# Moving a relu, a set of block sums and a row maximum by one place in the written order of a one-core graph-network kernel

## The chip, the cores and the metric

The kernel runs on one core of one Trainium2 chip. The metric is the device time of one execution in microseconds (us). A core has engines that run side by side, each through its own list of instructions: TensorE multiplies matrices (PE in the profile; PEld is the loading of its stationary operand), VectorE works elementwise (DVE), ScalarE does copies, exponentials and other activations (ACT), GpSimd does small work here (POOL), and SyncE issues the DMA transfers (SP). They wait for each other through semaphores.

## The reference

Two layers run over 16 graphs ("batches") of 1,024 nodes with 512 features. Layer 0 is an adjacency product and a weight product, layer 1 a graph attention with a masked softmax. Both start with a layer norm and a relu and end in a residual.

```
def _layernorm(x, axis=-1, eps=1e-5):
    m = jnp.mean(x, axis=axis, keepdims=True)
    v = jnp.var(x, axis=axis, keepdims=True)
    return (x - m) / jnp.sqrt(v + eps)

# --- layer 0 ---
h = jnp.maximum(_layernorm(x, axis=-1), 0.0)
y = jnp.einsum('nm,bmd->bnd', adj, h)
x = x + (jnp.einsum('bnd,do->bno', y, weight) + bias)
# --- layer 1, mask = adj ---
u = jnp.maximum(_layernorm(x, axis=-1), 0.0)
h = jnp.einsum('bnc,cf->bnf', u, W)
s1 = jnp.einsum('bnf,f->bn', h, a[:F, 0])
s2 = jnp.einsum('bnf,f->bn', h, a[F:, 0])
e = jax.nn.leaky_relu(s1[:, :, None] + s2[:, None, :], negative_slope=0.2) * mask
att = jax.nn.softmax(e, axis=2)
x = x + jax.nn.elu(jnp.einsum('bij,bjf->bif', att, h) + beta * h)
```

Shapes: x (16, 1024, 512), adj and mask (1024, 1024), weight and W (512, 512), all float32. (The reference calls both normed inputs h; u is the kernel's name for the second.)

## The kernel before

**Products.** Every matrix product is split into 2 x 2 blocks and done with seven block products instead of eight (Strassen's scheme in Winograd's form, `PRODUCTS`): p1 to p7, whose left operands are A11, A12, A22 and the sums S1 to S4, and whose right operands are B11, B21, B22 and the sums T1 to T4. The results are accumulated in three kinds of PSUM banks, Y, W and X. In layer 0, from batch 1 on, each of the seven products is split once more into seven inner products r1 to r7 (`inner_steps`, line 197). Their left sums are made on VectorE by `inner_left` (line 435), four additions of 128 x 256 each; they are the `in_p` tiles. In the trace r1, r6 and r7 of product p3 are the matmuls that write `y_p3y`, and r5 shares their PSUM tile `yx`: r1, r6 and r7 use its first half, r5 its second half. After r1 ScalarE copies the first half out (`y_p3t`), after r5 it copies the second half into the left sums' tile (`in_p`), and after r6 VectorE adds these two (`y_p3t<-y_p3y,in_p`); r7 writes the first half anew. The names are the same for p7, p4 and, in layer 1 where only p4 is split again, for `z_p4y` and `z_p4t`.

**Layer 0** (`layer0_a2`, line 451, through `products_a2`, line 300) runs for each batch in 28 steps, numbered 0 to 27. Products go in pairs, p1 with p2 (steps 0 to 6), p6 with p5 (7 to 13), p7 with p3 (14 to 20), then p4 with the first weight product woven in (21 to 27); then the other six weight products follow (`po_Y`, `po_X`, `po_W` in the trace). In a pair the two products' inner products alternate, two to a step: p7 r1, p7 r2 | p3 r1, p7 r5 | p3 r2, p7 r4 | p3 r5, p7 r6 | p3 r4, p7 r3 | p3 r6, p7 r7 | p3 r3, p3 r7. In the first step of a pair the last results of the pair before are read out (the list `behind`): for p5 these are two ScalarE copies of the X banks (`y_C<-y_X`).

**Side work.** After step k of a batch, `after(k)` issues whatever a table lists for k. For layer 0 the table is `plan_out` (line 1151) merged with others. It finishes the previous batch: the residual rows (`xr`) are normalized into u, statistics (`o.stats`), relu (`o.relu`, two ScalarE activations of 128 x 512 in place), the attention logits (`o.logits`, VectorE), and the stores. `inner_left` of p7, p3 and p4 and the loads of residual rows stand in the same table. `plan_norm_a` adds the next batch's norm statistics (`h_stats`, ScalarE, from step 15 on).

**Layer 1** (`layer1`, line 910, through `products_a`, line 275) takes 12 half-product steps 0 to 11 (p1, p2, p6, p5, p7, p3 with two steps each), then p4 in seven steps with a weight product woven in, then the other weight products (`pq_*`). Beside batch b's products runs the softmax of batch b+1 (`SOFTMAX_A`, line 1202): `M` masks a row block on VectorE and takes its maxima, `X` sends the maxima through DRAM to the other partitions (`mall`), `N` takes the first half's maxima from them (`top`, two small VectorE instructions that make `nm`), `E` is the exponential on ScalarE, which needs `nm`, and `V` transposes on VectorE. `LATE_A` (line 1209) makes T3 and T4, the last right sums of batch b: VectorE additions of 128 x 1024, one for each half, "a" and "b". p7 reads T3, p4 reads T4. In batch 0 `w_sums` makes the sums of the second weight matrix, four additions of 128 x 512.

**Order.** All engines are wrapped in `InOrder` (line 111), which keeps the order of the program on each of them; a table entry's place therefore is its place in the queue of each engine that it uses. `merged` (line 1119) appends the plans' entries for one step in the order in which the plans are passed.

Of the kernel before, what the change touches and what calls it, by code (L numbers as in the profile page):

```python
# [66 lines left out]
def kernel(  # L67
# [34 lines left out]
    def bank(name):  # L102
        return psum.tile([P, 512], F32, tag="ps", name=name)
# [232 lines left out]
    class Weighted:  # L336
# [17 lines left out]
        def steps(self, n, left):  # L354

            prod, _, bn, kind, first, last = self.products[n]
            first = first and (kind, 0) not in self.banks

            def step(q, i, dc):
                if first and i == 0 and dc == 0:  # L360
                    self.banks[kind, q] = bank(f"{self.name}_{kind}{q}")
                ps = self.banks[kind, q].rearrange("p (i o) -> p i o", i=2)
                pe.matmul(
                    ps[:, i, :], left[:, dc, ts(2 * q + i, P)], self.w[:, W_BLOCK[bn], dc, :],
                    start=(first and i == 0 and dc == 0), stop=(last and dc == 1),
                    skip_group_check=True,
                )
                if i and dc:
                    self.done(prod, q, ps)

            return [partial(step, q, i, dc) for q in range(2) for i in range(2) for dc in range(2)]
# [10 lines left out]
    def load_w(name, src):  # L382

        w = const.tile([P, 7, 2, HD], F32, tag="w", name=name)
        for i in range(2):
            for j in range(2):
                sp.dma_start(
                    out=w[:, 2 * i + j],
                    in_=src[ts(i, HD), ts(j, HD)].rearrange("(c p) o -> p c o", p=P),
                )  # L390
        return w
# [727 lines left out]
    def merged(*plans):  # L1119
        out = {}  # L1120
        for plan in plans:
            for k, steps in plan.items():
                out.setdefault(k, []).extend(steps)
        return out
# [26 lines left out]
    def plan_out(o, b):  # L1151

        return steps(
            (-1, o.keep, 0, 1), (-1, o.keep, 1, 0), (-1, o.keep, 1, 1), (0, o.relu, 0, 0),
            (1, o.stats, 1, 0, 0), (3, o.relu, 0, 1), (4, o.stats, 1, 0, 1), (7, o.relu, 1, 0),
            (8, o.stats, 1, 1, 0), (10, o.stats, 1, 1, 1), (13, o.relu, 1, 1),
            (2, o.logits, 0, 0, 0), (3, o.logits, 0, 0, 1), (7, o.logits, 0, 1, 0),
            (8, o.logits, 0, 1, 1), (9, o.logits, 1, 0, 0), (10, inner_left, b, "p7"),
            (12, o.logits, 1, 0, 1), (13, inner_left, b, "p3"), (15, o.logits, 1, 1, 0),
            (16, o.logits, 1, 1, 1), (16, o.store_logits), (18, inner_left, b, "p4"),  # L1160
            (3, o.store, 0, 0), (6, o.store, 0, 1), (10, o.store, 1, 0), (15, o.store, 1, 1),
            (18, begin, b, "Y"), (24, begin, b, "X"),
            (8, load_res, b, 0, 0), (10, load_res, b, 0, 1), (14, load_res, b, 1, 0),
            (18, load_res, b, 1, 1),
        )
# [16 lines left out]
    def plan_softmax(order, s):  # L1182
        names = {
            "L": [s.logits], "B": [s.blocks, 0], "b": [s.blocks, 1],
            "X": [s.spread_max, 0], "x": [s.spread_max, 1], "N": [s.top, 0], "n": [s.top, 1],
            "S": [s.spread_sum, 0], "s": [s.spread_sum, 1],
            "D": [s.diagonal, 0], "d": [s.diagonal, 1],
        }
        for g in range(NCH):
            names[f"M{g}"] = [s.masked, g]  # L1190
            names[f"E{g}"] = [s.exp, g]
            names[f"V{g}"] = [s.turn, g]
            names[f"L{g}"] = [s.load, g]
            names[f"e{g}"] = [s.load, g, b4, "b4"]
            names[f"K{g}"] = [s.keep, g]
            names[f"R{g}"] = [s.reload, g]
        for n in ("T1", "T2", "T3", "T4"):
            for k in range(2):
                names[n + "ab"[k]] = [s.right_sum, n, k]
        return {k: [tuple(names[n]) for n in steps.split()] for k, steps in order.items()}  # L1200
# [5 lines left out]
    }  # L1206
    SOFTMAX_B = {1: "D", 2: "T1a", 3: "T1b", 4: "d", 5: "T2a", 6: "T2b"}
    LOGITS_B = {8: "L", 9: "L0", 10: "L1", 11: "e2", 12: "e3"}
    LATE_A = {5: "T3a T4a", 6: "T3b T4b"}


    EARLY_B = {
# [18 lines left out]
    sms = [Softmax(b) for b in range(B)]  # L1231
    out_of = None
    for b in range(B):
        plans = [plan_out(out_of, b)] if b else []
        plans_b = []
        if b + 1 < B:
# [21 lines left out]
        if b == 0:  # L1258
            plan_b = merged(
                {  # L1260
                    0: [(logit_weights_back, 0), (logit_weights_back, 1)],
                    1: [(inner_right, "p7", 1)], 2: [(inner_right, "p3", 1)],
                    3: [(inner_right, "p4", 1)],
                },
                *plans_b,
            )
            layer0_a(b, merged(plan_first(), at_end(merged(*plans))))
        else:
            plan_b = merged(*plans_b)
# [9 lines left out]
    w1_c = load_w("w1_c", w1)  # L1279
    for b in range(B):  # L1280
        plans = [{
            k - 14: [(f,) for f in later.pop(k)] for k in sorted(later)
        }]
        plans.append(plan_softmax(LATE_A, sms[b]))
        plans.append(steps((7, p4_right, b, 0), (8, p4_right, b, 1), (8, p4_left, b)))
        plans.append(steps((3, u_sums, b, 0, 1), (4, u_sums, b, 1, 1)))
        plan_b = {}
        if b == 0:
            plans += [
                {6: [(w_sums, w1_c)]}, steps((-1, u_sums, b, 0, 0), (0, u_sums, b, 1, 0)),  # L1290
            ]
        if b + 1 < B:
            plans.append(plan_softmax(SOFTMAX_A, sms[b + 1]))
            plans.append({k: [(load_u, b + 1, n)] for k, n in LOADS_U.items()})
            plan_b = plan_softmax(SOFTMAX_B, sms[b + 1])
        else:
            plans.append({7 + i: [(load_x1, b, nh, q)] for i, (nh, q) in enumerate(halves)})
        if b + 2 < B:
            plan_b = merged(plan_b, plan_softmax(LOGITS_B, sms[b + 2]))
        if 1 <= b <= NCH:  # L1300
            plan_b = merged(plan_b, {
                4: [(late.load, b - 1)], 9: [(late.stats,)], 10: [(late.relu,)],
                11: [(late.logits, b - 1)], 13: [(late.store,)],
            })
            if b == NCH:
                plan_b[13].append((late.store_logits,))
        if b + 1 < B:
            plan_b = merged(plan_b, steps((10, u_sums, b + 1, 0, 0), (12, u_sums, b + 1, 1, 0)))
        plans.append({18: plan_b.pop(1, [])})
        layer1(b, merged(*plans), plan_b)  # L1310
    for k in sorted(later):
        for f in later[k]:
            f()
# [33 lines left out]
```

## Time and profile before

| quantity | before |
|---|---|
| time, median of 3 runs | 2254.78 us (2254.56 to 2255.46) |
| the profiled execution's own time | 2254.63 us |
| its span, first to last instruction | 2252.7 us |
| PE busy | 2236.1 us, 99% |
| PEld, DVE, ACT, POOL busy | 73%, 87%, 69%, 11% |
| granted TensorE clock | 0.998 |
| DMA, mean | 149 GB/s |

The span leaves out 1.93 us of the execution around the program's instructions. Times in the trace are counted from the start of the span. All instructions carry line 119, that of the wrapper `InOrder`, so that they are told apart by their tiles: what is written stands left of the arrow, what is read right of it, with buffer numbers left out. A matmul row "x4" is one inner product. In square brackets is the time that the engine stood idle before a row, and what ended it.

### The profile page before, as it was taken

To read this page: it belongs to the slowest core of one execution; us is meant where nothing else is said; L and a number is where in the kernel's file an instruction comes from. 1 tells how busy PE (TensorE), PEld (TensorE's weight loads), DVE (VectorE), ACT (ScalarE), POOL (GpSimd) and SP (SyncE) were. 2 spreads that over 40 slices of the span, in tenths; PEclk is the share of its full clock that TensorE was granted. 3 is DMA by queue.
4 is the path that set the end of the run, shared out by engine and by line. 5 is a ranking of instruction groups with operands and counts; after the bars stand their busy time and mean duration, and the time that the engine had idled before them with its cause. 6 is when DMAs were issued, how large, how long until landed. Compare 5 with 4: busy or idle time off the path is not lost.

```text
span 2252.7 us, 30436 instructions
## 1 busy us (share of the span) xinstructions
PE 2236.1 (99%) x8716; PEld 1645.5 (73%) x8716; DVE 1950.3 (87%) x4477; ACT 1547.9 (69%) x4138; POOL 243.7 (11%) x508
## 2 busy tenths in 40 slices
PE   9999999999999999999999999999999999999998
PEld 5888888888888888888666556665666556665565
DVE  7888888998888998898989988898889988888864
ACT  3766766676777676776576777768777776767743
POOL 1211111111111111111000000000000000000000
PEclk9999999999999999999999999999999999999999
DMA  7433454443444343344535665465554655446541
GB/s 210 140 126 119 160 171 132 141 140 117 148 160 151 134 142 120 120 150 159 202 110 175 165 169 166 145 196 156 164 168 149 191 142 153 139 143 165 159 120 49
DMA packets 194296, 336.07 MB, mean 149 GB/s; under 512 B 78800, under 2 KB 86992, under 8 KB 194128
## 3 DMA queue, kind: packets, MB, share of 16 engines
q1 hardware_dynamic: 185168, 302.15, 41.2%
q0 software_dynamic: 8640, 31.46, 7.5%
q8 instruction: 68, 1.11, 0.2%
q14 instruction: 100, 0.82, 0.1%
q10 hardware_dynamic: 320, 0.52, 0.1%
HBM read 228.33 MB, written 109.91 MB: 150 GB/s over the span
## 4 chain that ended last, share of the span: by engine, by line
PE 96%; DVE 2%; ACT 1%; DMA 1%; issue 0%; POOL 0%; SPq 0%; DVEq 0%; POOLq 0%
PE z_Y L119 16%; PE po_Y L119 10%; PE pq_Y L119 9%; PE z_X L119 9%; PE y_Y L119 8%; PE po_X L119 5%; PE z_W L119 5%; PE pq_X L119 5%; PE y_X L119 4%; PE y_W L119 3%; PE y_p7y L119 2%; PE pq_W L119 2%; PE po_W L119 2%; PE z_p4y L119 2%; PE y_p3y L119 2%; PE y_p4y L119 2%
## 5 line engine op out<-in xcount | busy, mean ns | idle before, releaser
L119 ACT ACTIVATE e<-e,nm 128x256 f32<-128x256 f32 x480 | 236.8, 498 | 51.4 <-DVE nm L119 51.4
L119 DVE CUSTOM_DVE_ANT_0 e<-e,mask 128x256 f32<-128x256 f32 x512 | 199.9, 424 | 54.0 <-ACT e L119 52.8
L119 PE MATMUL z_Y<-pT,ul_U 128*128 128x512 f32 x512 | 224.9, 592 | 0.0
L119 ACT ACTIVATE e<-s2b,s1b 128x256 f32<-128x256 f32 x512 | 214.7, 500 | 0.0
L119 PE MATMUL pq_Y<-w_c,z_C 128*128 128x256 f32 x768 | 189.1, 379 | 0.0
L119 PE MATMUL po_Y<-w_c,y_C 128*128 128x256 f32 x768 | 188.3, 379 | 0.0
L119 PEld LDWEIGHTS z_Y<-pT,ul_U 128*128 128x128 f32 x512 | 97.3, 190 | 115.6 <-issue 111.5
L119 DVE CUSTOM_DVE_ANT_0 y_S<-xr,v_bc 128x512 f32<-128x512 f32 x240 | 165.3, 689 | 9.2 <-DVE s L119 0.5
L119 PEld LDWEIGHTS po_Y<-w_c,y_C 128*128 128x128 f32 x768 | 145.9, 190 | 20.3 <-ACT po_X L119 0.2
L119 PEld LDWEIGHTS pq_Y<-w_c,z_C 128*128 128x128 f32 x768 | 145.9, 190 | 19.9
L119 DVE STREAM_TRANSPOSE pT<-e 128x512 f32<-128x512 f32 x240 | 150.8, 680 | 1.5
L119 ACT ACTIVATE h<-h,nb_h,r_h 128x512 f32<-128x512 f32 (+1 forms) x132 | 98.2, 792 | 57.1 <-POOL nb_h L119 57.1
L119 ACT ACTIVATE y_S<-xr 128x512 f32<-128x512 f32 x90 | 56.7, 630 | 91.9 <-DVE xr L119 91.5
L119 POOL DMA_DIRECT2D o<-x1d x60 | 52.7, 935 | 609.7 <-DVE o L119 546.8
L119 PE MATMUL pq_X<-w_c,z_S 128*128 128x256 f32 x512 | 115.9, 379 | 0.0
L119 PE MATMUL po_X<-w_c,y_S 128*128 128x256 f32 x512 | 115.7, 379 | 0.0
L119 PE MATMUL z_W<-pT,ul_U 128*128 128x512 f32 x256 | 112.5, 592 | 0.0
L119 PE MATMUL z_Y<-pT_T,ul_S 128*128 128x512 f32 x256 | 112.5, 592 | 0.0
L119 PE MATMUL z_X<-pT_T,ul_S 128*128 128x512 f32 x256 | 112.5, 592 | 0.0
L119 PE MATMUL z_X<-pT,ul_S 128*128 128x512 f32 x256 | 112.5, 592 | 0.0
L119 PEld LDWEIGHTS pq_X<-w_c,z_S 128*128 128x128 f32 x512 | 96.3, 190 | 14.5 <-DVE z_C L119 0.8
L119 PEld LDWEIGHTS po_X<-w_c,y_S 128*128 128x128 f32 x512 | 97.3, 190 | 13.2
(259 smaller groups left out, 5238.3 us busy)
## 6 DMA issues: line engine op xcount, KB each, us to landing
mask<-maskd SPq DMA_DIRECT2D x128, 512.0 KB
h<-in_x_dram SPq DMA_DIRECT2D x64, 512.0 KB
xr<-in_x_dram SPq DMA_DIRECT2D x256, 128.0 KB
x1d<-xr SPq DMA_DIRECT2D x64, 512.0 KB
ul_U<-ud_U SPq DMA_DIRECT2D x64, 512.0 KB
ud_U<-xr SPq DMA_DIRECT2D x60, 512.0 KB
o<-x1d POOLq DMA_DIRECT2D x60, 512.0 KB, 8.0
out_dram<-o SPq DMA_DIRECT2D x240, 128.0 KB
```

Of the source, the lines that this page charges most:

```text
L119: return lambda *args, **kwargs: tc.keep_in_program_order(f(*args, **kwargs))
```

## The change

Three entries move.

- Layer 0, in `plan_out`: the relu of u's last chunks (node half 1, quarter 1) goes from step 13 to step 14, and `inner_left` of p4 from step 18 to step 17. Both apply to batches 1 to 15.
- Layer 1: the second halves "T3b T4b" leave `LATE_A` for a plan `LATE_A2` of their own for the same step 6, which is merged last. At step 6 the queue of VectorE then has `N` ahead of T3b and T4b; before, it came behind them.
- Layer 1, batch 0: `w_sums` goes from step 6 to step 7, where it comes behind the first part of `p4_right`.

```
-            (8, o.stats, 1, 1, 0), (10, o.stats, 1, 1, 1), (13, o.relu, 1, 1),
+            (8, o.stats, 1, 1, 0), (10, o.stats, 1, 1, 1), (14, o.relu, 1, 1),
...
-            (16, o.logits, 1, 1, 1), (16, o.store_logits), (18, inner_left, b, "p4"),
+            (16, o.logits, 1, 1, 1), (16, o.store_logits), (17, inner_left, b, "p4"),
...
-    LATE_A = {5: "T3a T4a", 6: "T3b T4b"}
+    LATE_A = {5: "T3a T4a"}
+    LATE_A2 = {6: "T3b T4b"}
...
         plans.append(plan_softmax(LATE_A, sms[b]))
+        late_a2 = plan_softmax(LATE_A2, sms[b])
...
-                {6: [(w_sums, w1_c)]}, steps((-1, u_sums, b, 0, 0), (0, u_sums, b, 1, 0)),
+                {7: [(w_sums, w1_c)]}, steps((-1, u_sums, b, 0, 0), (0, u_sums, b, 1, 0)),
...
-        layer1(b, merged(*plans), plan_b)
+        layer1(b, merged(*plans, late_a2), plan_b)
```

## The prediction

> **What bounds the kernel.** I read the page first, then who waits for whom, then the timeline around each wait.
>
> ```profile
> PE 2236.1 (99%) x8716; PEld 1645.5 (73%) x8716; DVE 1950.3 (87%) x4477; ACT 1547.9 (69%) x4138; POOL 243.7 (11%) x508
> ```
>
> TensorE is the bound: 16.6 us of 2252.7 are not matmul. Only breaks in its stream can be won. The waits of the weight loads tell which moved entry touches one:
>
> ```profile
> PEld y_p7y L119 <- ACT y_p7t L119: 6.5, 15, 0.4
> PEld y_p3y L119 <- DVE y_p3t L119: 5.9, 15, 0.4
> ...
> PEld pq_X L119 <- DVE z_C L119: 0.8, 3, 0.4
> ```
>
> The first two come once in each of batches 1 to 15 of layer 0. In layer 1 the pq_X wait and one of z_p4y for ACT z_p4t (1.6, once) matter in batch 0 alone. Now batch 7 of layer 0 in the timeline, TensorE, then ScalarE, then VectorE:
>
> ```profile
> 518.83 1.03 PE L119 MATMUL y_p3y<-adjT_B,hS 128*128 128x256 f32 x4
> 519.88 1.13 PE L119 MATMUL y_p7y<-ext,in_p 128*128 128x256 f32 x4
> 520.85 1.03 PE L119 MATMUL y_X<-adjT_B,hS 128*128 128x256 f32 x4
> ...
> 527.76 1.03 PE L119 MATMUL y_X<-adjT_B,in_p 128*128 128x256 f32 x4
> 528.78 1.13 PE L119 MATMUL y_p3y<-adjT_B,hS 128*128 128x256 f32 x4
> 529.75 1.03 PE L119 MATMUL y_p4y<-adjT_T,h 128*128 128x256 f32 x4
> ```
>
> ```profile
> 518.04 1.52 ACT L119 ACTIVATE xr<-xr,nb_u,r_u 128x512 f32<-128x512 f32 x2
> 519.47 0.36 ACT L119 COPY y_p7t<-y_p7y 128x256 f32<-128x256 f32 x1
> 519.72 1.09 ACT L119 COPY y_C<-y_X 128x512 f32<-128x512 f32 x2
> 520.67 0.41 ACT L119 COPY y_p3t<-y_p3y 128x256 f32<-128x256 f32 x1
> ...
> 531.63 0.36 ACT L119 COPY y_p4t<-y_p4y 128x256 f32<-128x256 f32 x1
> ```
>
> ```profile
> 526.23 0.70 DVE L119 TENSOR_TENSOR y_Y<-y_Y,y_p7t 128x512 f32<-128x512 f32 x1 [1.23 <-PE y_Y L119]
> 526.84 0.42 DVE L119 TENSOR_TENSOR in_p<-h 128x256 f32<-128x256 f32 x1
> ...
> 528.30 0.42 DVE L119 TENSOR_TENSOR y_p3t<-y_p3y,in_p 128x256 f32<-128x256 f32 x1
> ```
>
> An undisturbed inner product takes 0.86 us (529.75 to the next matmul at 530.61). 518.83 to 519.88 and on to 520.85 is 0.19 and 0.11 too long: p7 r5 waits for the copy of p7 r1, which stands on ScalarE behind the relu. 527.76 to 528.78 to 529.75 is 0.16 and 0.11 too long: p3 r7 waits for the addition of p3 r6, which stands on VectorE behind p4's left sums. Together 0.57 us. The period agrees: p7 r1 begins at 450.06 and 517.10, 67.04 us apart, and 49 inner products of 0.863 with 7 weight products of 3.453 make 66.47.
>
> [...] r5's load begins at 519.88, 0.05 after the copy's end. [...] Here a load runs one matmul (0.22 us) ahead; p7 r5's was 0.41 late and cost 0.30, so the first 0.11 of a late load is free. [...] the trace has 1.43 for the two relu (518.04 to 519.47). [...] SyncE's row of maxima issued at 1558.08 lets its reader issue at 1560.19.
>
> None of the moved entries issues a DMA or uses POOL.
>
> **Relu to step 14.** p7's copy now comes directly when p7 r1 has ended (517.10 + 1.03 = 518.13), 1.3 us before it is needed: 0.30 won. What is queued behind the relu now? The two `y_C<-y_X` copies stay ahead of it; the second waits for its VectorE addition (end 519.68) and starts at 519.72 in any case. Relu 520.20 to 521.63, then p3's r1 copy, 0.36, to 521.99, ready 522.04. p3 r5 starts undisturbed at 517.10 + 6 x 0.863 = 522.28, its load at 522.06. It fits by 0.02, and by 0.13 with the free part: cost 0, bounds 0 and 0.15. Further back, the next batch's statistics start 0.82 later; ScalarE's idle 0.52 and 1.25 before its rows at 523.64 and 527.96 absorb it, without that cover the p7 r7 copy would be late. The logits of the moved chunk need the first relu's end, 521.02, when VectorE reaches them (521.05). SyncE's store of this u goes from 520.32 to about 521.7; the next entry there waits for logits until 523.35 anyway, so no load moves.
>
> **p4's left sums to step 17.** Four additions, 526.84 to 528.30, 1.46 us. At step 17 they follow the r6 addition of 524.58 and fill 524.92 to 526.38, the 1.23 idle before 526.23. The p7 r3 addition then comes at 526.38, p3's r6 addition at 526.99 to 527.41 (r6 itself ends at 526.76); r7's load is due at 528.10. 0.27 won with 0.65 to spare. VectorE then waits for ScalarE's p7 r7 copy and runs on from 528.06 instead of 528.64.
>
> **Late next: p4 r5.** ScalarE runs without a break from the p7 r7 copy (527.96) to p4's r1 copy (531.63 to 531.99). That chain starts only 0.30 earlier, since p7 r7 lies ahead of the second gain, while TensorE is 0.57 earlier. The copy is ready at 531.74; r5's load is due at 532.34 - 0.57 - 0.22 = 531.55. Late by 0.19, cost 0.08; bounds 0 and 0.19. So 0.49 a batch, 14 batches: 6.9 us.
>
> **Batch 15** has exponentials and transposes of graph 0 in these steps. There the X additions come late (1056.38, behind a transpose), the `y_C` copies at 1057.14, and p3 r2 waits for the first of them until 1057.78 whatever the relu does. So p7's 0.30 is lost again; the relu ends at 1059.59, p3's copy is ready at 1060.00 against a load due at 1059.39, cost 0.50; p3 r7's 0.27 is won. Net +0.2 us.
>
> **Layer 1, batches 1 to 15.** In the batch of 1528.42:
>
> ```profile
> 1553.60 1.22 DVE L119 TENSOR_TENSOR pT<-pT,pT 128x1024 f32<-128x1024 f32 x1
> ...
> 1555.87 0.25 DVE L119 TENSOR_REDUCE nm<-mall 128x16 f32<-128x64 f32 x1
> ```
>
> `N` goes to 1553.60, E0 from 1556.37 to about 1554.1, T3b and T4b end 0.37 later, at 1556.2. p7's third chunk reads T3b at about 1557.6, and the sum of VectorE's work is the same; it meets TensorE again at 1566.38 after 0.59 idle. No matmul of these batches waits for an exponential: 0. N's new wait, for the maxima, is covered: the last packet ends at 1552.07, the tightest batch has 1.06 us, of which its signal takes about 0.6 (the second row of maxima's last packet ends at 1559.58, its reader issues at 1560.19). The last batch has no next softmax: nothing moves.
>
> **Layer 1, batch 0** takes 73.24 us against 71.42: r5 of p4 waits 1.24 for a ScalarE copy behind late exponentials (1.50 lost with its restart), and pq_X loses 0.33 (0.59 and 3.62 in place of 0.43 and 3.45). N moves from 1128.08 to 1123.27, past `w_sums` (2.6) and T3b, T4b (2.3), so r5's wait goes. But VectorE has no idle time from 1114.26 to the addition that frees pq_X's bank (`z_C<-z_Y,z_p4t`, 1149.66 to 1150.35; pq_X begins at 1150.41). All moved work stays ahead of it; only the 0.1 before the first transpose (1130.68) goes. The stall moves to pq_X. -0.1, bounds 0 and -1.8.
>
> **Sum.** -6.9 + 0.2 - 0.1 = -6.8. The profiled execution took 2254.63 (span 2252.7 and 1.93 around it), so 2247.8; it lies 0.15 below the median, so 2248.0.
>
> **Rivals.**
> - *The relu only hands the stall on.* As in batch 15, p3's copy comes 0.4 late and costs 0.30 each time. For: 0.02 us of slack by my sum. Against: 14 batches agree to 0.01 us. Then 0.27 - 0.08 remain, 14 x 0.19 = 2.7: 2252.1.
> - *More goes.* p4 r5 in time, batch 15 too, batch 0 free: 15 x 0.57 + 1.8 = 10.4: 2244.4. Against: VectorE's full queue in both.
> - *N blocks VectorE.* If `mall` is visible later than N's new place, T3b, p4's sums and the transposes queue behind it. Price: about 0.5 of arrival slack and 0.59 of idle are free, then pq_X pays 1:1 in 14 batches. It decides from (6.8 + 4.5)/14 = 0.8 beyond these, a landing 1.9 us later; at 2.3, 14 x 1.2 - 6.8 = +10: 2264.8. For: in three batches that idle is 0 to 0.29. Against: nothing moved on SyncE's queue ahead of that transfer.
> - *Nothing.* The named releasers aren't the last, another wait stands behind: 2254.8.
>
> **How the numbers follow.** 0.68 for the forecast (own range 2246.4 to 2249.8), 0.16 handed on, 0.05 more, 0.05 blocked, 0.06 nothing. The range 2246.4 to 2253.0 holds the first two, 0.84. A measurement of this kernel tells 0.2%, 4.5 us, from no change: faster is below 2250.3. Faster 0.68 + 0.05 + 0.02 of the second, 0.75; same 0.14 + 0.06, 0.20; slower 0.05.
>
> **What would show it.** Right: the two PEld waits fall to one time or none; the period of layer 0 is 66.5 to 66.6; a small wait of y_p4y for y_p4t appears; batch 0 of layer 1 keeps 73.1 with its wait on pq_X for z_C; E0 starts 2.3 us earlier. Wrong: a PEld wait of y_p3y for ACT y_p3t in all batches, or DVE idle before nm.

## The result and the profile after

The changed kernel takes 2248.1 us (median of 8 runs, 2247.52 to 2250.28) against 2254.76 us before (8 runs, 2254.36 to 2256.19). The ratio is 0.9971, 95% interval 0.996 to 0.9982: 6.7 us, 0.29%, faster. The prediction was 2248.0 us. The profiled execution has a span of 2245.6 us at a granted clock of 0.998, 7.1 us less than before.

The line of the page with each engine's busy time and instructions, kernel after:

```profile
PE 2229.6 (99%) x8716; PEld 1648.6 (73%) x8716; DVE 1948.1 (87%) x4477; ACT 1551.3 (69%) x4138; POOL 245.0 (11%) x508
```

The same instructions are issued; TensorE is still the bound. Its recorded busy time falls by 6.5 us of the 7.1, and the rest of the span only from 16.6 to 16.0 us. So the 16.6 us that the prediction read off the page as not matmul are not the measure of what can be won. A row is recorded at 1.03 us while the next one can start after 0.86, so that a short stall lies under the recorded time of the row before it: in the prediction's lines the row of 518.83 ends at 519.86, and the stalled one starts at 519.88. The two rows of before that follow a late load, at 519.88 and 528.78, are themselves recorded at 1.13. The gain has to be looked for in the waits. The list of who waits for whom, kernel after, weight loads (total us, times, longest us):

```profile
PEld y_p4y L119 <- ACT y_p4t L119: 2.6, 14, 0.3
...
PEld z_p4y L119 <- ACT z_p4t L119: 1.3, 1, 1.3
PEld pq_X L119 <- DVE z_C L119: 1.2, 4, 0.5
...
PEld y_p3y L119 <- ACT y_p3t L119: 0.6, 1, 0.6
```

The two waits of 6.5 us and 5.9 us, 15 times each, are gone. New is one of `y_p4y` for ScalarE's copy of p4's r1, 14 times. p3 waits for its own copy once only, and that is batch 15.

Batch 7 of layer 0 (p7 r1 begins at 514.09) in the timeline: start in us from the start of the span, duration, engine. TensorE, kernel after:

```profile
516.68 1.03 PE L119 MATMUL y_p7y<-ext,in_p 128*128 128x256 f32 x4
517.54 1.03 PE L119 MATMUL y_X<-adjT_B,hS 128*128 128x256 f32 x4
...
525.32 1.03 PE L119 MATMUL y_p3y<-adjT_B,hS 128*128 128x256 f32 x4
526.18 1.03 PE L119 MATMUL y_p4y<-adjT_T,h 128*128 128x256 f32 x4
...
528.77 1.08 PE L119 MATMUL y_p4y<-ext,in_p 128*128 128x256 f32 x4
529.68 0.59 PE L119 MATMUL po_Y<-w_c,y_C 128*128 128x256 f32 x2
```

p7 r5 (516.68) and p3 r7 (525.32) are followed by the next product 0.86 us later: nothing is lost there any more. p4 r5 (528.77) is followed after 0.91. ScalarE in the same batch, kernel after:

```profile
515.15 0.37 ACT L119 COPY y_p7t<-y_p7y 128x256 f32<-128x256 f32 x1
...
517.18 1.52 ACT L119 ACTIVATE xr<-xr,nb_u,r_u 128x512 f32<-128x512 f32 x2
518.61 0.35 ACT L119 COPY y_p3t<-y_p3y 128x256 f32<-128x256 f32 x1
...
528.30 0.36 ACT L119 COPY y_p4t<-y_p4y 128x256 f32<-128x256 f32 x1
```

The copy of p7's r1 now stands ahead of the relu, and p3's copy directly behind it: it ends at 518.96, and p3 r5 starts at 519.27 without a break. VectorE, kernel after:

```profile
522.85 0.42 DVE L119 TENSOR_TENSOR in_p<-h,in_p 128x256 f32<-128x256 f32 x1
523.18 0.69 DVE L119 TENSOR_TENSOR y_Y<-y_Y,y_p7t 128x512 f32<-128x512 f32 x1
523.86 0.43 DVE L119 TENSOR_TENSOR y_p3t<-y_p3y,in_p 128x256 f32<-128x256 f32 x1
```

The last of p4's four left sums (522.85) now lies ahead of p7's addition and of p3's r6 addition; the latter ends at 524.29 against a load of p3 r7 due at about 525.10 (525.32 less 0.22).

Where the 7.1 us of span went, worked out from the starts of p7 r1 in layer 0 and of the first matmul of each batch in layer 1:

| stretch | before | after | difference |
|---|---|---|---|
| one batch of layer 0 (13 such periods) | 67.03 | 66.52 (one 66.60) | -0.51 |
| the 14th period, up to p7 r1 of batch 15 | 67.52 | 67.01 | -0.51 |
| last p7 r1 to the start of layer 1 | 44.19 | 44.48 | +0.29 |
| start of layer 1, from the start of the span | 1098.05 | 1091.26 | -6.79 |
| batch 0 of layer 1 | 73.24 | 73.01 | -0.23 |
| batch 6 of layer 1 | 71.42 | 71.71 | +0.29 |
| last batch of layer 1, to the end of the span | 81.58 | 81.25 | -0.33 |

Layer 0 has nearly all of it. Batch 3 of layer 1 took 71.46 before and 71.42 after, and the other batches 71.42 in both. The last row isn't the change's: the two runs below that leave layer 1 as it was took 81.52 (the relu alone) and 81.15 (the left sums alone) there. What decides between the two stayed open. Batch 0 varies too, which is taken up below.

### The profile page after: what moved, and what is told of

The parts are those of the page before. It is cut to its first block, busy times and chain, and to the rows that moved or that the text cites. A ratio compares the mean times of both kernels' runs of the same rounds, so it can differ in the third digit from the quotient of the medians.

```text
span 2245.6 us, 30403 instructions
## 1 busy us (share of the span) xinstructions
PE 2229.6 (99%) x8716; PEld 1648.6 (73%) x8716; DVE 1948.1 (87%) x4477; ACT 1551.3 (69%) x4138; POOL 245.0 (11%) x508
## 4 chain that ended last, share of the span: by engine, by line
PE 94%; DVE 3%; DMA 1%; ACT 1%; issue 0%; SPq 0%; POOL 0%; DVEq 0%; ACTq 0%; POOLq 0%
PE z_Y L119 15%; PE pq_Y L119 9%; PE po_Y L119 9%; PE z_X L119 9%; PE y_Y L119 8%; PE pq_X L119 5%; PE po_X L119 5%; PE z_W L119 5%; PE y_X L119 4%; PE y_W L119 3%; PE pq_W L119 2%; PE z_p4y L119 2%; PE po_W L119 2%; PE y_p3y L119 2%; PE y_p7y L119 2%; PE y_p4y L119 2%
```

## Experiments

Each "before" below is the unchanged kernel on the same chip in the same session (2254.87 us for the first four, 2254.92 for the last four).

### The relu alone

The kernel before, with one of the entries moved.

```
-            ... (13, o.relu, 1, 1),
+            ... (14, o.relu, 1, 1),
```

> Theory A (two separate stalls, each removed by its own move): p7 r5 no longer waits for the p7 copy, p3 r7 keeps its wait for p3's r6 addition (about 0.27 us), p4 r5 has no new wait because ScalarE and TensorE move by the same 0.30. Period of layer 0 66.73 to 66.75 instead of 67.03; 14 x 0.30 = 4.2 won, batch 15 loses 0.3 to 0.5: about 2251.0. Rival B (the stall is only handed on to p3 r5): period near 67.0, 2254.5. Rival C (the gain of the whole change comes from layer 1): no change, 2254.8.

Measured: 2251.35 us (2250.68 to 2253.12), ratio 0.9983 (0.9977 to 0.999). The period of layer 0 is 66.73 us, 0.30 less than before. The list of waits, weight loads:

```profile
PEld y_p3y L119 <- DVE y_p3t L119: 5.9, 15, 0.4
```

p3's wait for VectorE is what it was before, p7's for its copy is gone, and no wait of p3 for ScalarE took its place, but for one of 0.6 us in batch 15. The end of layer 0 is 0.48 us longer (44.67). 14 x 0.30 - 0.48 = 3.7; measured 3.5. The rival "the relu only hands the stall on" wanted hardly any gain here.

### The left sums alone

```
-            ... (18, inner_left, b, "p4"),
+            ... (17, inner_left, b, "p4"),
```

> Theory A: p3 r7's wait goes (0.27), p7 r5's stays (0.30); p4 r5 now waits for ScalarE's copy of p4 r1, late by about 0.19 and costing 0.05 to 0.08, since TensorE is 0.27 earlier there and ScalarE's chain isn't. Period 66.81 to 66.83; 14 x 0.21 = 2.9 won: about 2251.8. Rival B (the two stalls are one chain, so that one without the other gives nothing): 2254.8. Rival C (layer 1 gives it): 2254.8.

Measured: 2251.68 us (2251.05 to 2253.67), ratio 0.9986 (0.998 to 0.9993); period 66.83 us, 0.20 less than before. The list of waits, weight loads:

```profile
PEld y_p7y L119 <- ACT y_p7t L119: 6.5, 15, 0.4
...
PEld y_p4y L119 <- ACT y_p4t L119: 2.6, 14, 0.3
```

p7's wait stays, p3's for VectorE is gone, and the new wait at p4 r5 is here in full, while the relu alone doesn't have it. It belongs to this edit: TensorE gets 0.27 us earlier at a place that ScalarE's chain doesn't follow. 0.30 and 0.20 make 0.50; both edits together give 0.51.

### The layer-1 part alone

The kernel after, with the relu back at step 13 and the left sums back at 18. T3b and T4b behind `N`, and `w_sums` at step 7, are both kept; the two were not tried apart.

```
-            ... (14, o.relu, 1, 1),
+            ... (13, o.relu, 1, 1),
-            ... (17, inner_left, b, "p4"),
+            ... (18, inner_left, b, "p4"),
```

> Theory A: layer 0 as before (67.03); batch 0 of layer 1 73.0 instead of 73.24, the other batches 71.42 with the exponentials 2.3 us earlier and nothing won: 2254.5. In a batch where the maxima land late N stalls VectorE by up to 1.2 us, and pq_X up to 0.4. Rival C (layer 1 gives the gain): 2250 or less. Rival D (N's wait for the maxima costs in every batch): 2258 or more.

Measured: 2254.27 us (2253.93 to 2256.63), ratio 0.9998 (0.9989 to 1.0006): not to be told from no change. Layer 0 has its old period of 67.03; batch 0 of layer 1 takes 73.00, batch 3 71.52, all others 71.42.

### The first maxima taken earlier still

This measures the rival "N blocks VectorE". In the kernel after, `N` goes from the start of step 6 to the end of step 4, where in none of the 15 batches the maxima have come yet.

```
-        4: "M5 M6", 5: "M7 x",
-        6: "N B E0",
+        4: "M5 M6 N", 5: "M7 x",
+        6: "B E0",
```

> The changed kernel with N further ahead, at the end of step 4, in front of T3a, T4a and the masking of the last block, so that it stands before its maxima have arrived in every batch. It measures the price of the wait that the change risks. Theory A (VectorE has 0.75 us of idle time before the p3 addition in a batch, what goes beyond is paid 1:1 by TensorE): N comes at 21.5 us of the batch, the maxima are visible at 24.0, wait 2.5, cost about 1.75 in each of 14 batches and 1.9 in batch 0: about 2248 + 26 = 2274 (2265 to 2282), with TensorE waiting at pq_X or for T3b. Rival E (the idle time of VectorE in the rest of the batch takes it up): 2248 to 2250.

Measured: 2273.43 us (2272.32 to 2273.64), ratio 1.0081 (1.0067 to 1.0095). The list of waits of VectorE, then of the weight loads:

```profile
DVE nm L119 <- DMA mall<-md: 35.3, 15, 3.1
```

```profile
PEld z_p4y L119 <- ACT z_p4t L119: 15.4, 15, 2.7
PEld z_Y L119 <- DVE pT L119: 13.7, 13, 2.0
PEld pq_X L119 <- DVE z_C L119: 9.4, 28, 0.5
```

VectorE stood still for 35.3 us in 15 batches, and the kernel became 25.3 us slower than the kernel after (2248.1). The prediction's price says: what exceeds VectorE's later idle time is paid 1:1. Batch by batch it holds. In eleven of the batches 1 to 14, with waits of 1.32 to 2.96 us, the batch is longer than 71.42 by its wait less 0.86 or 0.87. In batches 3, 4 and 5 only 0.29 to 0.49 is free; there VectorE had stood idle for some 0.7 to 1.1 us more than in the others already, before maskings, mostly for loads of the mask. The free 0.86 is more than the 0.59 of idle time that the prediction read; in the kernel after that idle time is 0.74 (batch 7). Batch 0 doesn't fit: it grew by 2.66 for a wait of 1.30, and why stayed open. Of the places where it is paid, pq_X was named by the prediction, and p7's first matmul that reads T3b (`z_Y` for `pT`) by the expectation; p4 r5 was not foreseen.

### The sums of the second weight matrix earlier

The kernel after, with `w_sums` of batch 0 at step 3.

```
-                {7: [(w_sums, w1_c)]}, ...
+                {3: [(w_sums, w1_c)]}, ...
```

> The changed kernel with w_sums at step 3 of layer 1's batch 0, where VectorE stands idle for 1.85 us waiting for an exponential's input on ScalarE, instead of step 7. Theory F (batch 0 is bound by VectorE's gapless queue, and r5's wait stayed because the second half's exponentials follow the second N, which stands on VectorE behind w_sums): VectorE is 1.85 us further in batch 0, r5's wait of 0.9 and pq_X's of 0.5 both go, batch 0 takes 71.4 to 71.6 instead of 73.0: 1.5 us won, 2246.6. Rival G (r5 waits for the length of ScalarE's own queue of exponentials): r5's wait stays at 0.9, batch 0 takes 72.5 to 73: 2247.9.

Measured: 2246.87 us (2245.76 to 2247.04), ratio 0.9962 (0.9949 to 0.9974). Timeline of VectorE:

```profile
1105.85 2.71 DVE L119 TENSOR_TENSOR w_c<-w_c 128x512 f32<-128x512 f32 x4
```

At this place the four additions delay nothing. Batch 0 takes 71.42 us, the time of the other batches; its waits at p4 r5 and pq_X are both gone. So those stalls came from VectorE's queue, in which these 2.6 us stood at the wrong place, and p4 r5's wait could be removed. The sums now fill an idle stretch of VectorE ahead of a masking, 1.74 us long in the kernel after. In this profile too batch 6 is longer, 72.12 us: VectorE waited 1.56 us there for the first maxima.

### All together

The kernel before's remaining stalls, taken away as the readings name them: `w_sums` at step 3, the first relu of the next batch's node rows (`h_relu`) one step later so that p4's copy doesn't stand behind it, and the moved relu at step 13 again in batch 15 alone.

```
-                (20, h_relu, b, 0), ...
+                (21, h_relu, b, 0), ...
...
-            ... (14, o.relu, 1, 1),
+            ... (14 if b + 1 < B else 13, o.relu, 1, 1),
...
-                {7: [(w_sums, w1_c)]}, ...
+                {3: [(w_sums, w1_c)]}, ...
```

> The changed kernel with three more moves: w_sums at step 3, the relu of h's first chunks from step 20 to 21, behind the copy that p4 r5 waits for, and in batch 15 the relu of u's last chunks back at step 13. Theory A: y_p4y's 14 waits for ACT y_p4t go, the period of layer 0 falls from 66.53 to 66.48 (0.7 us in all), batch 15 wins back 0.3, batch 0 of layer 1 1.5: 2245.6. Rival: the copy of r5 becomes late behind the relu and r6 waits for it: 2247 to 2250.

Measured: 2244.72 us (2244.58 to 2245.31), ratio to before 0.9953 (0.9939 to 0.9967): the fastest version, 10.2 us below before and 2.9 below the kernel after in the same session. TensorE at the place of p4 r5 in batch 7 of layer 0:

```profile
528.92 0.60 PE L119 MATMUL po_Y<-w_c,y_C 128*128 128x256 f32 x2
529.35 1.03 PE L119 MATMUL y_p4y<-ext,in_p 128*128 128x256 f32 x4
530.22 0.60 PE L119 MATMUL po_Y<-w_c,y_C 128*128 128x256 f32 x2
```

p4 r5 takes 0.87 (529.35 to 530.22), the wait for its copy is gone from the list, and the periods of layer 0 are 66.48, but for the last, up to batch 15, with 66.96: what the prediction worked out for 49 inner products and 7 weight products without a break, 66.47 (66.46 from its figures as printed). The end of layer 0 is 43.99, and all batches of layer 1 take 71.42.

### The kernel after once more

The kernel after unchanged, beside the two above and the one below.

> The changed kernel itself once more, as the mark for the other three: 2248.1, period of layer 0 66.53, batch 0 of layer 1 73.0.

Measured: 2247.58 us (2247.45 to 2248.35), ratio 0.9966 (0.9954 to 0.9979). Period 66.52. Batch 6 of layer 1 takes 71.42, without a wait for the maxima, but batch 0 takes 73.54 instead of 73.01: these two vary from one execution to the next.

### How much room the relu has at its new place

The kernel after, with the moved relu written as four activations of 128 x 256 instead of two of 128 x 512, to make p3's copy late.

```
-            self.norms[nh, q].relu()
+            for c in range(2) if nh and q else [None]:
+                self.norms[nh, q].relu(slice(None) if c is None else ts(c, HD))
```

> The changed kernel with the moved relu issued as four activations of 128 x 256 instead of two of 128 x 512, the same arithmetic, only longer on ScalarE, to see how near p3 r5 stands to a wait for p3's copy. Theory A (spare time 0.02, and 0.11 of a late load is free): four halves take about 1.6 to 2.0 us instead of 1.43, the copy is 0.2 to 0.6 later, p3 r5 waits in every batch and costs 0.07 to 0.45: a period of 66.6 to 67.0, 2249 to 2254.5. Rival H (r5 doesn't need that copy, or has much more time): period 66.53, 2248.1.

Measured: 2253.81 us (2253.4 to 2255.23), ratio 0.9994 (0.9986 to 1.0002); period 66.93. Timeline of ScalarE in batch 7, then of TensorE:

```profile
519.87 2.07 ACT L119 ACTIVATE xr<-xr,nb_u,r_u 128x256 f32<-128x256 f32 x4
521.85 0.35 ACT L119 COPY y_p3t<-y_p3y 128x256 f32<-128x256 f32 x1
```

```profile
521.09 1.03 PE L119 MATMUL y_Y<-ext,h 128*128 128x256 f32 x4
522.25 1.13 PE L119 MATMUL y_p3y<-ext,in_p 128*128 128x256 f32 x4
```

The four take 1.98 us (519.87 to 521.85) instead of 1.43, so the copy comes 0.55 later, and p3 r5 begins 1.16 after the product ahead of it instead of 0.86; the period grows by 0.41 (66.93 - 66.52). The list of waits, weight loads:

```profile
PEld y_p3y L119 <- ACT y_p3t L119: 8.7, 15, 1.2
```

The wait that the rival describes is the one that appears here, in all 15 batches. Without batch 15's 1.2 it is 7.5 / 14 = 0.54 each time: of the delay of 0.55 about 0.01 was spare in front of the load, and 0.54 - 0.41 = 0.13 more cost nothing. The slack was small, and it was there: 0.14 together, which the prediction put at 0.02 and 0.13 together.

## Why the prediction was right, and where a step was wrong

**Relu to step 14: right.** 0.30 was to be won per batch and p3 r5 to fit by 0.02, by 0.13 with the free part. The relu alone gave 0.30; the split relu shows a slack of 0.14 (0.55 later for a cost of 0.41). The rival that hands the stall on is refuted for batches 1 to 14; a copy more than 0.14 us later would have begun to cost, by an estimate from these two figures. That p7 r5 waits for the copy of p7 r1 is shown (15 waits, 6.5 us, before; none when the relu alone moves behind that copy); why it does so, though it writes the other half of the tile, no run tried.

**Left sums to step 17: right.** 0.27 was to be won; p3 r7 starts on time, with 0.8 to spare (0.65 predicted).

**Late next, p4 r5: right in mechanism, a little too dear.** The load waits 0.19 us each time (2.6 / 14), the lateness that was predicted. It costs 0.05 in place of 0.08: 0.91 - 0.86 in the timeline, and 66.52 - 66.48 when the wait is taken away. A batch of layer 0 therefore wins 0.51, not 0.49: 7.1 us instead of 6.9 in 14 batches.

**Batch 15: right in sign.** +0.2 was predicted, +0.29 measured (44.48 - 44.19). The runs part the two: the relu alone lengthens this stretch by 0.48 (44.67), near the predicted 0.50, and the left sums alone shorten it by 0.20 (43.99), less than the predicted 0.27. With the relu back at step 13 in this batch alone, the stretch takes 43.99.

**Layer 1, batch 0: near in the sum, wrong in the step.** "So r5's wait goes" failed. The weight load's wait of p4 r5 is 1.3 us after, against 1.6 before, and 1.8 in the second profile of the kernel after. The timeline of the kernel after, ScalarE and then TensorE:

```profile
1129.80 0.51 ACT L119 ACTIVATE e<-e,nm 128x256 f32<-128x256 f32 x1 [4.38 <-DVE nm L119]
```

```profile
1136.11 1.13 PE L119 MATMUL z_p4y<-ext,in 128*128 128x256 f32 x4 [0.91 <-ACT z_p4t L119]
```

ScalarE had done the first four exponentials long before, and stood idle for 4.38 us until `nm` of the second half of the maxima was made, which the change doesn't bring forward: it stands on VectorE behind `w_sums` and transposes. The copy that p4 r5 needs stands behind the exponentials of three of the four row blocks of that half (1129.80 to 1135.71). The prediction followed the first `N` and its exponentials, and took the whole 1.24 us of TensorE's idle time for theirs. What remained is 0.91 there, and 0.42 lost at pq_X instead of 0.33; the sum of batch 0 is -0.23 against a predicted -0.1, within its bounds of 0 and -1.8. But 0.23 by itself is not shown to be the change's. Over the profiles batch 0 takes 73.24, 73.39 and 73.69 with the old order of layer 1, and 73.00, 73.01, 73.17 and 73.54 with the new. In all but one of these it follows VectorE's idle time before one masking, for an exponential or a load of the mask (1.85, 2.02, 2.32; 1.74, 1.97, 2.35): it is that idle time plus 71.4 with the old order, plus 71.2 or 71.3 with the new. (The one is the layer-1 part alone, 73.00 with 1.38.) For the same idle time the new order is then 0.1 to 0.2 shorter, near what was predicted. That VectorE's full queue would keep the loss in batch 0 was right: it was set free (71.42 us) in the two runs that shorten the queue ahead of the second maxima by the sums at step 3.

**Layer 1, batches 1 to 15: right, but for one batch.** E0 was to start 2.3 us earlier: counted from the start of its batch it starts at 25.67 in batch 7 after (1618.73 - 1593.06), at 27.95 in batch 6 before (1556.37 - 1528.42). In this profile every batch in which `N` found its maxima there took 71.42. (Batch 3 takes 71.46 to 71.82 in four of the profiles, of either order; VectorE stands idle longer there before maskings.) In batch 6 of the kernel after it did not find them. VectorE, kernel after:

```profile
1546.53 0.08 DVE L119 DVE_READ_ACCUMULATOR2_ANT mx<- 128x1 f32 x1
1547.77 0.26 DVE L119 TENSOR_REDUCE nm<-mall 128x16 f32<-128x64 f32 x1 [1.15 <-DMA mall<-md]
```

This is the rival "N blocks VectorE", once in 15 batches. The transfer's packets end at 1546.67, 2.2 us after the last of its four issues ended, where about 1.0 is usual. The wait of 1.15 cost 0.29 in the period; the same batch in the run with the early sums waited 1.56 and cost 0.70. Both give a free part of 0.86, the same as with `N` at step 4. The prediction had said that a late landing decides from 0.5 + 0.59 + 0.8 on; a single one is small against 7 us. In the four other profiles of this order (layer-1 part alone, all together, the kernel after again, split relu) no first `N` waited. The packets in the traces point to why it is this batch. Near this transfer in batch 6, and in no other batch, there is a 16 KB packet of a queue that the page calls "instruction". In both late cases the last eight of the 512 packets of maxima begin just as that packet ends: it runs from 1545.17 to 1546.56 and they begin at 1546.55 (kernel after); it ends at 1545.70 and they begin at 1545.69 (early sums). In the other profiles the maxima had landed by the time that it began, or within 0.12 us of it. That the last packets stood behind it on one DMA engine is an estimate of the author's from these times and was not shown; the trace doesn't tell which engine carried them.

**The sum.** -6.9 + 0.2 - 0.1 was predicted. Measured in the profile: -7.1 + 0.3 = -6.8 in layer 0 (-6.79), and -0.3 in layer 1 made of batch 0, batch 3, batch 6 and the end of the last batch (-0.23 - 0.04 + 0.29 - 0.33). Of these only batch 6 is shown to be the change's in full. The medians differ by 6.7 us against a predicted 6.8. That layer 0 carries it was foreseen and is shown by the runs; that the time came to within 0.1 us of 2248.0 is in part luck, since batch 0 alone differs by 0.5 us between two profiles of the same kernel.

## What to carry to other kernels

When one engine is busy 99% of the time, as TensorE is here, list the waits of its loads by count: here each of the two waits that came once per batch was one entry in a written order, and the price was the lateness less 0.11 to 0.14 us. An entry that moves earlier can also make TensorE earlier for what follows (0.27 us with the left sums alone), so look for the next copy on an engine whose chain doesn't shift with it; here that is the copy for p4 r5, 0.19 us late. When a wait is to vanish because its cause moves, check every input of the waiting chain: here the copy hung on two row maxima, and only the first was moved.

## What the runs showed of the hardware

- The weight loads of these 128 x 256 products could come somewhat late for nothing: 0.19 us late cost 0.05 (p4 r5 after), 0.41 late cost 0.30 (p7 r5 before), 0.54 late cost 0.41 (p3 r5, split relu). The free part was 0.11 to 0.14 us, within the 0.22 us by which an undisturbed load ran ahead (before, p7 r1 in batch 7: the load begins at 516.88, its matmul at 517.10).
- The relu's activations in place took 0.495 us for 256 elements in a row (split relu, 1.98 / 4) and 0.715 for 512 (before and after, 1.43 / 2). An estimate from these two numbers is 0.275 us fixed and 0.86 ns an element.
- The same small transfer of maxima has its last packet 0.85 to 1.37 us after its last issue ended in 148 of the 150 cases in the ten profiles, and after 2.23 and 2.53 us in the two late ones. With its reader moved to about the moment at which it was usually there, VectorE waited for the late ones, 1.15 us (kernel after) and 1.56 us (early sums).
- TensorE's waits stood for the most part in its recorded busy time: with the span 7.1 us shorter (2252.7 to 2245.6), the busy time fell by 6.5 us (2236.1 to 2229.6).
